# Gated cross-attention with a low-rank expert layer, on one core: evenly spread products for K and V, another order of the sums, and another tail

## The chip, the core and the metric

The kernel runs on one core of one Trainium2 chip. A core has engines that run beside each other, each with its own queue in order: TensorE (PE) multiplies matrices into eight PSUM banks; VectorE (DVE) does elementwise work and reductions; ScalarE (ACT) does activations and copies; GpSimd (POOL) does elementwise work on SBUF, more slowly; SyncE (SP) issues most DMAs. The metric is the device time of one execution in microseconds (us), the median of several. All data is float32, and a float32 matmul runs as two passes, so that each matmul of the code is two matmul records in the trace.

## What is computed

```python
x = x + tanh(g_xattn) * attention(layernorm(x), ctx)      # x: 4 x 256 x 512, ctx: 4 x 1601 x 512
x = x + tanh(g_ffn)  * ffn(layernorm(x))

q = (query @ Wq + bq)            # 32 heads of 128, 4 query heads for each of 8 key/value heads
k, v = split(kv @ Wkv + bkv)     # 8 heads of 128
attn = softmax(q k^T / sqrt(128)); o = attn @ v; attention = o @ Wo + bo
ffn = x @ base_W^T + 2 * sum over the two best of 8 experts of w_e * (x @ A_e) @ B_e     # rank 16
```

## The kernel before

The work runs over 4 batches, 8 key/value heads each, and l = 0, 1 for the two halves of the 256 queries: 64 **groups** (b, h, l). A group has four query heads for 128 queries, that is 512 columns. The 1601 keys lie in 13 tiles: 12 of 128 and one of 65. They are handled in 7 units, the odd tile first and then six pairs.

For a group, `score_unit` makes the scores of a unit on TensorE (keys on partitions, 512 columns), and ScalarE copies them from PSUM into a `p` buffer, of which there are NBUF = 9. VectorE folds the units into a maximum (`fold`, L766 to L772). When all 7 are there, `softmax` runs `spread` on VectorE, which takes the maximum over partitions by two 32 x 32 block transposes, two reductions, and six copies of 32 x 16 between quadrants of partitions (L785 to L799). Then come, unit by unit, a subtraction on VectorE (L870), exp on ScalarE (L873), and the sum over units on VectorE. `av_unit` multiplies with the values; its sum stands in the one bank of `ps_av`. `sum_spread` runs `spread` once more for the sums, with a reciprocal in it, and `normalize` divides (L961). Then ScalarE adds the bias of the values, and `out_steps` projects with `Wo` (L977); with the last head, `ffn_steps` follows.

`run_group(cur, prev)` lays the scores of one group between the value products of the one before. After it comes `window`, which fills TensorE while the maximum is spread. I call that stretch the **filling** behind a group. What goes in are `Task`s: q of the next head (four items), K and V of the next pair of heads, the projection of the previous group, transposes of the next batch's context, x and feed-forward steps. Each task has steps with a cost and a time of readiness, and some have a due group, from which `window` works out a credit.

K and V of a pair of heads are made by `pair_steps` with seven products of half size in place of eight (Strassen-Winograd): sums of context columns (`ctx_sums`, tile `T`, VectorE) and of weights (`weight_sums`, four additions on GpSimd, L291) go in, and the results are copied by ScalarE and added up by VectorE (L676). V is made for two heads in one tile `v`, one buffer; weights of K and of V share one buffer `wkv`.

Order is written by the program. `manual_schedule` keeps TensorE, VectorE and ScalarE in the order in which the code issues their instructions. The code decides this order by a planner: `clock` holds a planned time for each engine, `queues` hold pieces of vector and scalar work with planned durations, `pump` issues the piece that can start first, and `force(key)` issues pieces until a certain one is out. A wait that the planner doesn't foresee stops everything behind it on that engine. Instructions of GpSimd and SyncE are placed by the framework.

Three places matter for what follows. Behind a group, before its accumulator is free, `av_unit` forces the spread of the sums and the normalization, ahead of the next maximum:

```python
        if j == NPAIR - 1 and key not in by_pe:
            force(("sums", key))
            normalize(key, force(("rb", key)))
```

V of a pair is due at once, behind the first group of the pair (h even, l = 0); K of the next pair is due over three groups (h even, l = 1, to h odd, l = 1). And the tail lays out the last group by itself: its scores, then everything that is left, then the two last groups' value products one after the other. In the tail the sums of the last two groups are made on TensorE with a matrix of ones (`su`), and the reciprocal is taken over 128 x 512 (L941).

Of the kernel before, what the change touches and what calls it, by code (L numbers as in the profile page):

```python
# [27 lines left out]
def flamingo_kernel(  # L28
# [89 lines left out]
    SEM = 200  # L118
    NEVER = math.inf
# [23 lines left out]

    def pump(until=NEVER, most=None):

        n = 0
        while most is None or n < most:
            heads = [(start_of(q[0]), i, q) for i, q in enumerate(queues.values()) if q]
            if not heads:
                return n  # L150
            start, _, q = min(heads)
            engine, ns, _, fn, key = q[0]
            if start == NEVER or start + min(ns, 1200) / 2 > until:
                return n
            q.popleft()
            fn()
            clock[engine] = start + ns
            if key is not None:
                done[key] = start + ns + SEM
            n += 1  # L160
        return n

    def force(key):

        while key not in done:
            assert pump(most=1), key
# [27 lines left out]
    bias = const.tile([NBIAS, P], F32, name="bias")  # L194
    biasT = const.tile([P, NBIAS], F32, name="biasT")

    def load_small():
        nc.scalar.dma_start(bias[0:NHEAD], bq.rearrange("(h p) -> h p", p=P))
        nc.scalar.dma_start(bias[NHEAD:], bkv.rearrange("(h p) -> h p", p=P))
# [4 lines left out]
    def turn_bias():  # L204
        pb = bank("pb")
        nc.tensor.transpose(pb[:, :NBIAS], bias, ident[:NBIAS, :NBIAS])
# [50 lines left out]
    w_t = {}  # L257

# [24 lines left out]
    def weight_sums(kind, b, hp):  # L283
        w = w_t[kind, b, hp]
        for out_, x_, y_, op in (
# [5 lines left out]
            nc.gpsimd.tensor_tensor(w[:, out_], w[:, x_], w[:, y_], op)  # L291

# [50 lines left out]
    STAGE = 3  # L343

    LAG_DMA, LAG_CTX, LAG_X = 2500, 1500, 3000
# [178 lines left out]
    def new_v(b, hp):  # L524
        v_t[b, hp] = pool.tile([P, KT, 2, HDIM], F32, tag="v", name=f"v_{b}_{hp}", bufs=1)
# [40 lines left out]
    def plain_v_steps(b, hp):  # L566
# [3 lines left out]
        def item(i):  # L570
# [3 lines left out]
            def run():  # L574
                w = w_t["v", b, hp]
                pv = bank(f"pv_{b}_{hp}_{i}")
                for j in range(n):
# [14 lines left out]
                nc.scalar.copy(  # L592
                    v_t[b, hp][:r, i : i + n].rearrange("p j t f -> p (j t f)"), pv[:r, : n * WV]
                )
                give(act(585))
# [4 lines left out]
    def pair_steps(kind, b, hp):  # L600
# [48 lines left out]
        def places(f, half, s, n, bk):  # L649

            if is_k:
# [6 lines left out]
                    v_t[b, hp][:, lo : lo + n // P, f, :],  # L658
# [21 lines left out]
        def step(i, s, n):  # L680
# [24 lines left out]
            if i == 1:  # L705
                ready = ("T", b)
# [15 lines left out]
        def tail():  # L722
            over()
            bk = bank(f"pt{nm}")
            for f in range(2):
# [8 lines left out]
            nc.scalar.copy(  # L734
                v_t[b, hp][:REST, FULL].rearrange("p t f -> p (t f)"), bk[:REST, : 2 * HDIM]
            )
            give(act(400))

        def over():
            left[0] -= 1  # L740
            if not left[0]:
                done["pair", kind, b, hp] = clock["now"]

# [4 lines left out]
        else:  # L748
            new_v(b, hp)
            cols = [(HT + s, SUB) for s in range(0, HK, SUB)]  # L750
        parts = [[step(i, s, n) for i in (1, 2, 6, 7, 5, 3, 4)] for s, n in cols]
        if REST and not is_k:
            parts.append([(2 * NC * BLOCK_COST, ("T", b), tail, True)])
# [23 lines left out]
    def spread(acc, op, nm, after=None):  # L777
# [4 lines left out]
        res = pool.tile([P, W], F32, tag=f"res_{op}", name=f"res_{nm}", bufs=1)  # L782

        def quadrants():
# [3 lines left out]
            for a in range(1, 4):  # L788
                nc.vector.tensor_copy(q[:32, a, :], q[32 * a : 32 * a + 32, 0, :])

        def whole():
# [3 lines left out]
            for a in range(1, 4):  # L795
                nc.vector.tensor_copy(m[32 * a : 32 * a + 32], m[:32])

        def back():
# [4 lines left out]
        return res, [  # L803
            (690, lambda: nc.vector.tensor_tensor(acc[:, 0, :], acc[:, 0, :], acc[:, 1, :], op)),
            (710, lambda: nc.vector.transpose(acc[:, 1, :], acc[:, 0, :])),
            (1240, quadrants),
            (1070 if after is not None else 800, whole),
# [3 lines left out]
    def score_unit(key, j):  # L811
# [15 lines left out]
        else:  # L827
            p = pool.tile([P, 2, W], F32, tag="p", name=f"p_{nm}_{j}", bufs=NBUF)
# [19 lines left out]
    acc_t, sum_t, late = {}, {}, []  # L848
    last = (B - 1, NKV - 1, NL - 1)
    by_pe = [(B - 1, NKV - 1, l) for l in range(NL)]  # L850
    assert (NPAIR - 1) * 2 * W <= NC * 2 * HW

    def softmax(key):
# [4 lines left out]
        mb, parts = spread(acc_t[key], ALU.max, f"mx_{nm}")  # L858
        for ns, fn in parts:
# [21 lines left out]
        if key not in by_pe:  # L881
# [8 lines left out]
    def sum_spread(key):  # L890

        rb_t[key], parts = spread(
            acc_t[key],
            ALU.add,
            f"sm_{'_'.join(map(str, key))}",
            lambda m: nc.vector.reciprocal(m, m),
        )
        for i, (ns, fn) in reversed(list(enumerate(parts))):
            end = ("rb", key) if i == len(parts) - 1 else None
            queues["sum"].appendleft(("v", ns, 0.0, fn, end))  # L900
# [476 lines left out]
```

## Time and profile before

| what | value |
|---|---|
| median of 3 runs | 2723.4 us (2721.6 to 2724.55) |
| the profiled execution | 2725.56 us |
| its span, first to last instruction | 2723.8 us |
| mean granted TensorE clock | 0.985 |
| GpSimd: weight additions L291 | 60 for V, 88.4 us; 60 for K, 70.5 us |
| VectorE: copies of 32 x 16 for the sums (L789, L796) | 186 of 164 ns and 186 of 166 ns |
| VectorE: copies of 32 x 16 for the maximum | 192 of 164 ns and 192 of 166 ns |
| VectorE: reciprocal over 128 x 512 in the tail | 2 of 3358 ns |

Stretches of the span, from the profile's windows (columns: stretch, its length, busy time of each engine with its number of records, granted clock, share and rate of DMA):

```profile
0.00:74.00 74.00, 62.67 (x262) 45.62 (x263) 18.22 (x30) 17.80 (x35) 9.25 (x27) 1.00 0.37 123
74.00:110.00 36.00, 32.62 (x91) 16.54 (x92) 25.78 (x34) 21.05 (x32) 0.00 (x0) 0.91 0.22 63
640.00:705.00 65.00, 54.22 (x139) 27.39 (x137) 52.42 (x83) 24.54 (x37) 3.16 (x3) 0.89 0.08 25
2622.00:2724.00 102.00, 79.44 (x180) 34.80 (x178) 66.30 (x122) 27.91 (x40) 0.00 (x0) 0.88 0.05 16
110.00:640.00 530.00, 522.77 (x1810) 294.84 (x1809) 442.81 (x659) 242.74 (x386) 33.36 (x25) 1.00 0.12 39
```

The engines stand in the order PE, PEld (weight loads of TensorE), DVE, ACT, POOL. The first stretch is the start, up to the first scores; the second holds groups 0 and 1; the third is the change from the first batch to the second; the last is the tail. A wait is written as "who line <- whom line", with its sum, its number and the longest.

### The profile page before, as it was taken

How to read it: one execution, taken by the hardware profiler on the slowest of the kernel's cores; microseconds unless marked ns; L12 is line 12 of the kernel's file. 1: busy time of each engine (PE TensorE's matmuls, PEld its weight loads, DVE VectorE, ACT ScalarE, POOL GpSimd, SP SyncE). 2: the span in 40 equal slices, each digit the busy share in tenths (PEclk: the TensorE clock that was granted, in tenths of full speed). 3: DMA queues.
4: the chain of work that ended last, by engine and by line, in shares of the span. 5: the costliest groups of instructions: out<-in, count | busy, mean ns of one | idle time of the engine just before them, and what ended most of it. 6: DMA issues, size and time to landing. Idle time of an engine off the chain costs nothing.

```text
span 2723.8 us, 25225 instructions
## 1 busy us (share of the span) xinstructions
PE 2633.5 (97%) x9107; PEld 1486.4 (55%) x9107; DVE 2181.4 (80%) x3355; ACT 1207.4 (44%) x1898; POOL 165.7 (6%) x146
## 2 busy tenths in 40 slices
PE   8999999999999999999899999999989999999997
PEld 6546565564655646555365555656546564565643
DVE  2688787888778878788787887888877888888885
ACT  2444444445444344446354444454544444444441
POOL 0001000000000001000010000101000000000000
PEclk9999999999999999999899999999989999999998
DMA  3201001120111011102010111001110111111000
GB/s 128 61 24 38 31 24 39 39 88 0 39 43 39 24 43 47 31 24 87 16 47 22 36 51 39 24 31 42 57 39 24 35 32 35 39 33 37 24 16 8
DMA packets 78261, 104.70 MB, mean 38 GB/s; under 512 B 3324, under 2 KB 36140, under 8 KB 78136
## 3 DMA queue, kind: packets, MB, share of 16 engines
q1 hardware_dynamic: 76728, 102.01, 11.8%
q8 instruction: 72, 1.18, 0.2%
q0 software_dynamic: 272, 0.53, 0.1%
q10 hardware_dynamic: 1136, 0.55, 0.1%
q14 instruction: 53, 0.43, 0.0%
HBM read 100.98 MB, written 2.10 MB: 38 GB/s over the span
## 4 chain that ended last, share of the span: by engine, by line
PE 78%; DVE 16%; ACT 3%; issue 1%; DMA 1%; SPq 0%; ACTq 0%; DVEq 0%
PE av L912 21%; PE sc L834 20%; PE po L977 8%; PE pq L504 8%; PE pxk L629 5%; DVE p L870 3%; PE pyk L629 3%; DVE sm L772 3%; PE pyv L640 3%; ACT p L841 2%; DVE mx L772 2%; PE pxv L640 2%; PE pzk L629 1%; PE ptv L727 1%; PE py L1029 1%
## 5 line engine op out<-in xcount | busy, mean ns | idle before, releaser
L912 PE MATMUL av<-p,v 65*128 65x512 f32 x1640 | 775.1, 598 | 27.2 <-ACT p L873 27.2
L834 PE MATMUL sc<-qT,kT 128*128 128x512 f32 (+1 forms) x1664 | 782.4, 597 | 2.3 <-ACT qT L511 2.3
L841 ACT COPY p<-sc 65x512 f32<-65x512 f32 x820 | 467.9, 587 | 585.0 <-PE sc L834 417.9
L912 PEld LDWEIGHTS av<-p,v 65*128 65x128 f32 x1640 | 312.2, 192 | 412.1 <-issue 372.5
L834 PEld LDWEIGHTS sc<-qT,kT 128*128 128x128 f32 (+1 forms) x1664 | 309.7, 187 | 388.2 <-issue 361.7
L873 ACT ACTIVATE p<-p 65x512 f32<-65x512 f32 x442 | 428.1, 994 | 191.7 <-DVE p L870 187.3
L870 DVE TENSOR_TENSOR p<-p,res_mx 65x512 f32<-65x512 f32 x442 | 498.3, 1180 | 0.0
L772 DVE TENSOR_TENSOR mx<-mx,p 128x1024 f32<-128x1024 f32 x252 | 308.7, 1225 | 234.6 <-ACT p L841 231.0
L772 DVE TENSOR_TENSOR sm<-sm,p 128x1024 f32<-128x1024 f32 x252 | 316.2, 1255 | 7.2
L977 PE MATMUL po<-wo,oT 128*128 128x512 f32 x512 | 239.5, 612 | 15.2 <-DMA wo<-in_L_xattn_Wo_dram 12.4
L504 PE MATMUL pq<-xnT,wq 128*128 128x256 f32 x1024 | 235.0, 379 | 0.0
L504 PEld LDWEIGHTS pq<-xnT,wq 128*128 128x128 f32 x1024 | 193.5, 190 | 50.9 <-issue 18.4
L291 POOL TENSOR_TENSOR wv<-wv 128x256 f32<-128x256 f32 x60 | 88.4, 1492 | 1738.5 <-DMA wv<-in_L_xattn_Wkv_dram 1737.3
L667 ACT ACTIVATE kT<-pxk,biasT 128x384 f32<-128x384 f32 (+2 forms) x150 | 75.8, 526 | 264.4 <-PE pxk L629 264.4
L977 PEld LDWEIGHTS po<-wo,oT 128*128 128x128 f32 x512 | 98.9, 197 | 124.1 <-issue 113.9
L511 ACT ACTIVATE qT<-pq,biasT 128x256 f32<-128x256 f32 x128 | 60.5, 473 | 158.2 <-PE pq L504 158.2
L670 ACT COPY v<-pxv 128x384 f32<-128x384 f32 x120 | 56.5, 476 | 148.3 <-PE pxv L640 148.2
L766 DVE TENSOR_TENSOR mx<-p,p 128x1024 f32<-128x1024 f32 x63 | 77.5, 1230 | 48.7 <-ACT p L841 48.2
L291 POOL TENSOR_TENSOR wk<-wk 128x256 f32<-128x256 f32 x60 | 70.5, 1195 | 523.4 <-DMA wk<-in_L_xattn_Wkv_dram 397.0
L984 DVE SCALAR_TENSOR_TENSOR xa<-po,gates,xa 128x512 f32<-128x512 f32 x64 | 47.9, 749 | 62.5 <-PE po L977 62.4
L629 PE MATMUL pxk<-ctxT,wk 128*128 128x417 f32 (+1 forms) x240 | 90.5, 499 | 0.0
L640 PE MATMUL pxv<-wv,T 128*128 128x128 f32 x720 | 90.5, 276 | 0.0
(158 smaller groups left out, 2395.0 us busy)
## 6 DMA issues: line engine op xcount, KB each, us to landing
wq<-in_L_xattn_Wq_dram SPq DMA_DIRECT2D x32, 1024.0 KB, 5.2
wo<-in_L_xattn_Wo_dram SPq DMA_DIRECT2D x32, 1024.0 KB, 5.3
ctx<-in_ctx_dram SPq DMA_DIRECT2D x48, 256.0 KB, 2.7
wk<-in_L_xattn_Wkv_dram SPq DMA_DIRECT2D x30, 256.0 KB, 2.8
wv<-in_L_xattn_Wkv_dram SPq DMA_DIRECT2D x30, 256.0 KB, 3.0
xa<-in_x_dram SPq DMA_DIRECT2D x4, 512.0 KB
out_dram<-y SPq DMA_DIRECT2D x8, 256.0 KB, 2.0
base<-in_L_ffn_base_W_dram SPq DMA_DIRECT2D x4, 256.0 KB, 9.3
```

The costliest lines, as they stand in the source:

```text
L291: nc.gpsimd.tensor_tensor(w[:, out_], w[:, x_], w[:, y_], op)
L504: nc.tensor.matmul(pq[:, :L], w_t["q", b, h][:, c, g * HDIM : (g + 1) * HDIM], xnT_t[b][:, c, :], start=(c == 0), stop=(c == NC - 1),)
L629: nc.tensor.matmul(bk[:, :n], a(SLOT[i], c), operand(i, c, s, n), start=first and c == 0, stop=c == 1, skip_group_check=True,)
L640: nc.tensor.matmul(bk[:, t * HDIM : (t + 1) * HDIM], operand(i, c, s + t * P, P), a(SLOT[i], c), start=first and t == 0 and c == 0, stop=c ...
L766: nc.vector.tensor_tensor(acc, p[first], p[first + 1], op)
L772: nc.vector.tensor_tensor(acc, acc, p[j], op)
L834: nc.tensor.matmul(sc[:r, :], kT_t[b, h][:, key_col(i) : key_col(i) + r], qT_t[b, h][:, :, l * P : (l + 1) * P], start=True, stop=True,)
L841: nc.scalar.copy(p[:r, k, :], sc[:r, :])
L870: nc.vector.tensor_tensor(p, p, m, ALU.subtract)
L873: nc.scalar.activation(p, p, AF.Exp, scale=scale)
L912: nc.tensor.matmul(av, v_t[b, h // 2][:r, i, h % 2, :], p_t[key][j][:r, k, :], start=(j == 0 and k == 0), stop=(j == NPAIR - 1 and k == le ...
L977: nc.tensor.matmul(po, oT_t[key][:, g, :], w_t["o", b, h][:, g, :], start=(g == 0), stop=(g == G - 1),)
```

## The change

Seven things change together.

- **Sums.** `spread` gets an engine for its small copies: GpSimd for the sums, VectorE for the maximum as before. The planner lets 800 ns pass for three such copies (GP_COPIES). The spread result is written into the sums' own tile.
- **Normalization.** It is a piece in the queue of sums, forced only ahead of the next group's first value product.
- **The planner.** `force` finds the queue of the wanted piece, issues what stands before it there, and lets pieces of other queues of the same engine go first where they fit (FIT = 300).
- **K and V at an even rate.** V of the next pair is made from (h odd, l = 0) on and due by (h even, l = 0); chains share RATE = 10700 ns of TensorE in each filling, the older chain first. The next weights are loaded when the last product of the present ones is issued, and the products wait for them in the plan (LAG_PAIR). The values lie by head in a ring of three buffers. q of head 7 starts at l = 1.
- **Start.** K of the second head is a task in the first fillings.
- **Room.** Two staging buffers in place of three; the output is written over `x2`; `bias` lies in a buffer of `midT`.
- **Tail.** The last group's scores run between the value products of the one before (`run_group(last, prev, 4)`), its softmax starts as soon as they are out, and its value products are a task. Only the last group's sums are made on TensorE, and their reciprocal is taken on 128 x 16 between two transposes.

```diff
+    def take(q):
+        piece = q.popleft()
+        engine, ns, _, fn, key = piece
+        start = start_of(piece)
+        fn()
+        clock[engine] = start + ns
+        if key is not None:
+            done[key] = start + ns + SEM + (GP_COPIES if key[0] == "part" and key[2] < 4 else 0)
...
     def force(key):
         while key not in done:
-            assert pump(most=1), key
+            q = next((q for q in queues.values() if any(p[4] == key for p in q)), None)
...
+            engine, start = q[0][0], start_of(q[0])
+            for other in queues.values():
+                while other is not q and other and other[0][0] == engine:
+                    if start_of(other[0]) + other[0][1] > start + FIT:
+                        break
+                    take(other)
+            take(q)
...
-    STAGE = 3
-    LAG_DMA, LAG_CTX, LAG_X = 2500, 1500, 3000
+    STAGE = 2
+    LAG_DMA, LAG_CTX, LAG_X = 2500, 1700, 3000
...
-    def new_v(b, hp):
-        v_t[b, hp] = pool.tile([P, KT, 2, HDIM], F32, tag="v", name=f"v_{b}_{hp}", bufs=1)
+    def new_v(b, h):
+        v_t[b, h] = pool.tile([P, KT, HDIM], F32, tag="v", name=f"v_{b}_{h}", bufs=3)
...
             if i == 1:
-                ready = ("T", b)
+                ready = [("T", b), ("w", kind, b, hp)]
...
             for a in range(1, 4):
-                nc.vector.tensor_copy(q[:32, a, :], q[32 * a : 32 * a + 32, 0, :])
+                eng.tensor_copy(q[:32, a, :], q[32 * a : 32 * a + 32, 0, :])
...
-        rb_t[key], parts = spread(
+        rb_t[key] = acc_t[key][:, 0, :]
+        parts = spread(
             acc_t[key],
             ALU.add,
             f"sm_{'_'.join(map(str, key))}",
+            rb_t[key],
             lambda m: nc.vector.reciprocal(m, m),
+            nc.gpsimd,
         )
+        queues["sum"].appendleft(("v", 690, ("av", key), lambda: normalize(key), ("norm", key)))
         for i, (ns, fn) in reversed(list(enumerate(parts))):
-            end = ("rb", key) if i == len(parts) - 1 else None
-            queues["sum"].appendleft(("v", ns, 0.0, fn, end))
+            ready = 0.0 if i < 3 else ("part", key, i - 1)
+            queues["sum"].appendleft(("v", ns, ready, fn, ("part", key, i)))
...
+        if j == 0 and unfinished:
+            force(("norm", unfinished.pop()))
...
-        if j == NPAIR - 1 and key not in by_pe:
-            force(("sums", key))
-            normalize(key, force(("rb", key)))
+        if j == NPAIR - 1 and key != last:
+            done["av", key] = clock["now"] + SEM
+            unfinished.append(key)
...
-        nc.vector.reciprocal(rb, sum_t[key])
+        nc.vector.transpose(tr, sum_t[key])
+        give(vec(720))
+        nc.vector.reciprocal(m, tr.rearrange("p (c k) -> p c k", k=32)[:, :, 0])
+        nc.vector.transpose(
+            rb.rearrange("p (c k) -> p c k", k=32), m.unsqueeze(2).to_broadcast([P, NB, 32])
+        )
...
     def window(now):
+        left = RATE
...
+        for chain in sorted({t.chain for t in tasks if t.chain}):
+            some = [t for t in tasks if t.chain == chain]
+            cost = sum(t.cost() for t in some)
+            for t in some:
+                if t.due > now:
+                    t.credit = t.cost() * max(min(1, left / max(cost, 1)), 0)
+            left -= cost
...
-    for f in xs + vs + plain_k_steps(0, 1):
+    for f in xs + vs:
...
+    steps = plain_k_steps(0, 1)
+    steps.append((0, 0, lambda: last_sums(0)))
+    steps.append((0, 0, lambda: next_weights("k", 0, 1)))
+    tasks.append(Task(steps, 1))
...
-            if h % 2 == 0 and l == 0 and hi > 0:
-                tasks.extend(Task(part, now, True) for part in pair_steps("v", *pair))
...
-            if nxt is not None and l == (0 if nxt[1] > 0 else NL - 1):
+            if nxt is not None and l == (0 if 0 < nxt[1] < NKV - 1 else NL - 1):
                 tasks.append(Task(q_steps(*nxt), hi * NL + NL - 1))
...
+            if coming is not None and (h % 2, l) == (0, 1):
+                cb, cp = coming
+                steps = pair_steps("k", cb, cp, lambda c=coming: next_weights("v", *c))
+                tasks.append(Task(sum(steps, []), (hi | 1) * NL + NL - 1, now))
+            if coming is not None and (h % 2, l) == (1, 0):
+                cb, cp = coming
+                follow = next_pair(cb, cp)
+                then = None if follow is None else lambda f=follow: next_weights("k", *f)
+                for part in pair_steps("v", cb, cp, then):
+                    tasks.append(Task(part, (hi | 1) * NL + NL, now))
...
-    for j in range(NPAIR):
-        score_unit(last, j)
-    softmax(last)
-    flush(lambda t: True)
-    run_group(None, prev, 0)
-    tasks.insert(0, Task([sum_step(prev)] + out_steps(prev)))
-    run_group(None, last, 0, NEVER)
-    tasks.insert(0, Task(out_steps(last)))
+    run_group(last, prev, 4)
+    tasks.insert(0, Task(out_steps(prev)))
+    tasks.insert(0, Task([av_step(last, j) for j in range(NPAIR)] + out_steps(last)))
     flush(lambda t: True)
```

## The prediction

> **What bounds the kernel now.** I read the page's engine shares and chain first, then who TensorE waited for, then stretches of the timeline around the longest of these waits.
>
> ```profile
> span 2723.8 us, 25225 instructions
> PE 2633.5 (97%) x9107; PEld 1486.4 (55%) x9107; DVE 2181.4 (80%) x3355; ACT 1207.4 (44%) x1898; POOL 165.7 (6%) x146
> ...
> PE 78%; DVE 16%; ACT 3%; issue 1%; DMA 1%; SPq 0%; ACTq 0%; DVEq 0%
> ```
>
> TensorE bounds it, but 97% cannot be taken for a floor: records overlap and stretch when the clock falls. I count by starts instead. In undisturbed runs of the timeline a 512-column record starts every 0.429 us (eight of `po` at 864.12, the next at 867.56), a 256-column one every 0.216, a K product every 0.336 on average (0.350 and 0.322), a 128-column one every 0.112. The group list has 3950, 1128, 904 and some 3120 of them: 1695 + 244 + 304 + 349 = 2592 us. So 2723.8 - 2592 = 132 us is all that a better order can win. Where it lies, by TensorE's waits:
>
> ```profile
> PE av L912 <- ACT p L873: 27.2, 6, 6.5
> PE pyv L640 <- DVE v L676: 18.3, 12, 2.2
> PE po L977 <- DMA wo<-in_L_xattn_Wo_dram: 12.4, 3, 4.2
> PE pt_ctx L226 <- DMA ctx<-in_ctx_dram: 8.0, 4, 3.8
> PE pmt L1084 <- DVE mid L1074: 7.3, 2, 4.5
> PE pt_f L226 <- DVE fn L250: 4.8, 1, 4.8
> ```
>
> Columns: who, on whom, us in total, times, longest. The first and third row fall at the three batch boundaries. The first of them in the timeline:
>
> ```profile
> 643.79 1.45 PE L629 MATMUL pxk<-ctxT,wk 128*128 128x384 f32 x4
> 645.08 1.45 PE L629 MATMUL pzk<-ctxT,wk 128*128 128x384 f32 x4
> 646.38 2.74 PE L834 MATMUL sc<-qT,kT 128*65 128x512 f32 x6
> 655.64 2.08 PE L912 MATMUL av<-p,v 65*128 65x512 f32 x2 [6.53 <-ACT p L873]
> 657.51 3.62 PE L834 MATMUL sc<-qT,kT 128*128 128x512 f32 x4
> ...
> 685.74 1.45 PE L629 MATMUL pxk<-ctxT,wk 128*128 128x384 f32 x4
> 691.37 5.37 PE L977 MATMUL po<-wo,oT 128*128 128x512 f32 x8 [4.18 <-DMA wo<-in_L_xattn_Wo_dram]
> ```
>
> Behind group (head 7, l=0) the filling held only 5.4 us of K products (641.0 to 646.4), so TensorE ran dry for 6.5 us; after that four score records take 3.62 us where they take 1.88 elsewhere, the granted clock in 640 to 705 being 0.89. The projection postponed from there makes two projections in one filling, and the second waits 4.2 us for its weights.
>
> **The change part by part**, in us of span.
>
> *Products at an even rate.* Before, all V products of a pair (some 20 us) come behind one group, K in thirds behind three. After, both K and V are spread over all four fillings of a pair, at most 10.7 us each; K plus V of a pair is about 39.4 us by the starts above, or 9.9 per filling. In the burst, `pyv` accumulates and must wait for the vector add of an earlier part, which stood in VectorE's queue behind the sum and the maximum spread: 18.3 us in 12 waits. Half a burst with other pieces between has room for that add. Ends 0 and -18, taken **-14** (it is one wait per pair; I leave a quarter).
>
> *Batch boundary.* Per boundary: 6.5 of wait, 3.1 of slow records behind it (2.08, 3.62 and 2.22 against 1.02, 1.88 and 1.88), 4.2 for the weights of `po`, 1.8 of slow records: 15.6, or 47 for three. After, that filling gets K, and V of the next batch's first heads, to 10.7, plus a projection of 3.4; q of head 7 goes wholly into the filling before it. What is late next is the vector chain: in a usual boundary (855.3 to 866) sum spread 4.5, normalization 0.7, maximum spread 4.1, first subtraction 0.7 and exp 0.6, some 11 us. TensorE has the old group's last av records (3.4), the filling (14 and more) and three score tiles (2.6) against it: covered. The dry spell goes; the weights of `po` I count half gone, because the planner still knows no time for that load. 3 x (9.6 + 3.0) = **-38**, ends 0 and -47.
>
> *Start.* K of head 1 (10.8 us of products before the first scores) goes into the fillings behind groups 0 and 1, where TensorE waits 3.4 us for exp and then runs 4 score records in 3.62. **-6**, ends 0 and -8. Its weights load and additions are issued later with it, with a whole pair's time to spare.
>
> *Tail.* The four `su` records on the sums (1.7 us) go; two reciprocals over 128x512 of 3.36 us become transpose, small reciprocal, transpose (0.71 + 0.24 + 0.71 by their rows), for the last group; the other takes the usual path. Scores of the last group run between the av records of the one before, where TensorE now waits 1.3 and 3.0 us and then runs slow (2.9). The last serial piece (router, second product, output, from about 2697) stays. **-11**, ends -4 and -18.
>
> *Small copies on GpSimd.* Twelve copies of 0.165 us per group are on VectorE now; six move: 62 x 6 x 0.165 = 61 us of VectorE, which at 80% is not on the path, so nothing is gained directly. In exchange the second reduction and the last transpose each wait for three GpSimd copies, and behind a waiting vector instruction stand subtractions, maxima and the adds that K, V and ACT's score copies wait for. No such copy is in this trace; nearest are GpSimd memsets of 0.10 us, so three with their semaphores come to some 0.5 to 0.9 us. Here a rule speaks against the change. The row first:
>
> ```profile
> 70.26 2.89 POOL L291 TENSOR_TENSOR wk<-wk 128x256 f32<-128x256 f32 x4 [63.25 <-DMA wk<-in_L_xattn_Wkv_dram]
> ...
> 872.89 5.74 POOL L291 TENSOR_TENSOR wv<-wv 128x256 f32<-128x256 f32 x4 [116.20 <-DMA wv<-in_L_xattn_Wkv_dram]
> ```
>
> With VectorE idle four additions take 2.9 us; with VectorE on subtractions 5.7, and those subtractions go from 1.22 to 1.75. The Trainium skill, *SBUF — State Buffer*, "SBUF: two separate sides", says why: VectorE with two SBUF inputs and a GpSimd instruction that reads SBUF exclude each other for whole instructions. By the rule each of six copies could sit out one vector instruction of 1.2 us, 7.2 us per group of added latency; by the row, copies and vector instructions alternate only while VectorE has such an instruction ready, and as soon as it reaches the waiting reduction the copies run freely: one instruction of 1.2 us and then about 0.7, twice, or 3.8 per group less the 1.0 that the copies cost before, 2.8 us. The chain above is then 14 us against a cover of 20. I take the row: **+6** for the places where the cover is thin, ends 0 and +95 (1.5 in each of 63 groups).
>
> GpSimd also does the four weight additions for each of 30 loads (2 x 15), which stand until their DMA lands (3 us) and take 5.7. Copies behind them would come 6 to 9 us late, and the chain would be 20 to 23 against 20: it belongs to that upper end.
>
> *Normalization as a piece.* Its 0.69 us and the sum spread no longer have to come before the maximum spread, so exp of the next group can come up to 5 us earlier; but av's single accumulator makes the next group wait for it all the same. Counted within the boundary step.
>
> *Ring of three value buffers, split copies.* V of the next pair can start one group earlier than its last reader ends. ACT does 2 x 0.25 for 0.37 at each of 15 V ends, 2 x 0.37 for 0.56 at seven: about 3 us on an engine busy 44%. 0. *Two staging buffers for three:* a context load lands in 2.7 us and has two transposing steps of at least 1.7 between; 0, upper end +10. *Output in place of `y`:* 0.
>
> Sum: -14 - 38 - 6 - 11 + 6 = -63. On the profiled span, 2723.8 - 63 = 2661; its run was 2725.6, 1.8 around the span and 2.2 over the median of 2723.4. From the median: **2660**.
>
> **The rivals.**
>
> *Half of it* (0.22). The even rate works but the boundaries stay: context sums and K of the next batch become ready late, so the filling is bare whatever the rate allows, and `po` still meets its load. For it: 15.6 us at each boundary comes from readiness as much as from lack of work. Against: V is begun there too, where before it came a group later. -14 - 6 - 11 with +3: about 2695.
>
> *GpSimd turns the chain* (0.13, the other side). Place: the second reduction of the sums, VectorE waiting for copies which stand behind a vector instruction or behind weight additions whose DMA is not in. Price: what the chain exceeds its cover by. It decides from 69 us lost, 1.1 us per group over 63 groups, or 2.3 for each of 30 loads. For it: the rows above, and VectorE at 84% between 110 and 640. Against: the 6 us of cover to spare. At 1.5 per group: 2660 + 89 = 2749.
>
> *It does not spread* (0.06). Due dates and readiness push the products back into bursts; only the tail and a few us move: 2715, some of it within the bound for no change.
>
> **How the numbers follow.** My forecast has 0.59. A measurement of this kernel tells 0.2%, 5.4 us, from no change. Faster: 0.59 + 0.22 + half of the last, 0.84; same 0.03; slower 0.13. The range goes from 2632 (all the lower ends but some 10 us: 2592 of work, about 15 of filling the pipeline at the start, 20 of serial end) to 2712, which takes in the half case and costs of +50, and leaves out the slow side.
>
> **What would show it.** Right: no wait of `pyv` on VectorE's adds over 5 us in all; boundaries without a 6 us wait of `av` on exp and with clock 0.95 or more; tail from the last score record to the end shorter by 10; vector busy time down by about 60; `quadm` waits on GpSimd under 1 us each. Wrong: `av` or `sc` waiting about 1 us or more behind every group, released by a vector instruction that itself waited for GpSimd; GpSimd copies found behind the weight additions; or `po` still waiting for `wo` at each boundary.

## The result, and the profile after

The changed kernel takes 2961.3 us (median of 4 runs, 2958.1 to 2961.4), against 2722.7 us for the kernel before in the runs beside it: a ratio of 1.087, with a 95% interval of 1.085 to 1.089. The forecast was 2660. It is slower by 239 us where 63 less were expected.

The page of the changed kernel, its first lines and its chain:

```profile
span 2959.6 us, 25493 instructions
...
PE 2693.0 (91%) x9103; PEld 1501.9 (51%) x9103; DVE 2103.5 (71%) x2990; ACT 1210.5 (41%) x1914; POOL 219.5 (7%) x524
...
PE 83%; DVE 11%; POOL 3%; issue 1%; DMA 1%; ACT 1%; SPq 0%; POOLq 0%; DVEq 0%; ACTq 0%
```

TensorE has four records fewer than before and 236 us more of span. VectorE has become freer, as it should with the copies gone (2181 to 2104 us), and GpSimd is in the chain for the first time, with 3%. The busy time of TensorE is higher by 60 us for the same work, so a part of the loss is slow records. Who TensorE waited for tells where the rest is:

```profile
PE av L954 <- DVE oT L1005: 222.6, 37, 14.2
PE pt_x L249 <- DVE xn L273: 10.4, 4, 3.0
PE pt_ctx L249 <- DMA ctx<-in_ctx_dram: 6.9, 4, 3.5
PE av L954 <- ACT p L908: 4.7, 2, 2.6
```

One wait that did not exist before holds nearly the whole loss: value products of a group, 37 times, on `oT`, which is the normalization of the group before. The waits the change aimed at are gone from this list: `pyv` on VectorE (18.3), `po` on its weights (12.4), and most of `av` on exp (27.2).

To check that nothing else grew, I added up over the whole trace what lies between the start of a TensorE record and the next beyond the undisturbed spacing of its kind (0.429 us for 512 columns, and so on). The work itself is 2580 us before and 2578 after; the gaps are 136 and 374 us, a difference of 238. Gaps directly ahead of a group's first value product went from 28 to 231 us. Short ones, under 0.6 us, went from 36 to 93. Most of these lie where the clock was low: the trace has 33 stretches at half the clock, 279 us in all, where the kernel before has 12 with 84 us.

The place in the timeline, behind one ordinary group. Columns: start, duration, engine, line, operation, count, and in brackets the idle time before and what ended it.

```profile
198.03 0.68 DVE L835 TENSOR_TENSOR mx<-mx 128x512 f32<-128x512 f32 x1
...
201.61 0.71 DVE L829 STREAM_TRANSPOSE mb<-quadm_mx 128x512 f32<-128x512 f32 x1
...
203.53 1.81 DVE L905 TENSOR_TENSOR p<-p,mb 65x512 f32<-65x512 f32 x2
...
208.93 4.62 DVE L905 TENSOR_TENSOR p<-p,mb 128x1024 f32<-128x1024 f32 x4
...
212.43 2.79 PE L870 MATMUL sc<-qT,kT 128*65 128x512 f32 x6 [0.56 <-ACT qT L536]
212.56 4.08 POOL L315 TENSOR_TENSOR wv<-wv 128x256 f32<-128x256 f32 x4 [35.57 <-DMA wv<-in_L_xattn_Wkv_dram]
...
213.47 1.22 DVE L835 TENSOR_TENSOR sm<-sm 128x512 f32<-128x512 f32 x1
...
216.70 0.64 POOL L819 COPY quad_sm<-quad_sm 32x16 f32<-32x16 f32 x3
217.38 0.25 DVE L822 TENSOR_REDUCE quadm_sm<-quad_sm 32x16 f32<-32x64 f32 x1 [1.23 <-POOL quad_sm L819]
...
218.65 0.71 DVE L829 STREAM_TRANSPOSE sm<-quadm_sm 128x512 f32<-128x512 f32 x1 [0.75 <-POOL quadm_sm L826]
219.40 0.69 DVE L1005 TENSOR_TENSOR oT<-av,sm 128x512 f32<-128x512 f32 x1
...
220.14 2.08 PE L954 MATMUL av<-p,v 65*128 65x512 f32 x2 [4.92 <-DVE oT L1005]
```

VectorE's order is now: maximum spread (198.0 to 202.3), all seven subtractions with the additions of K between them (to 213.5), then the spread of the sums, then the normalization (done at 220.1). TensorE has run out of filling and of the three score tiles at 215.2. It stands for 4.9 us, though exp of the new group was ready since 204.9, and the two value records behind the wait take 2.08 us in place of 1.02. In the kernel before, the sums' spread and the normalization stood ahead of the maximum spread and of every subtraction (one place, from the normalization on):

```profile
821.37 0.69 DVE L961 TENSOR_TENSOR oT<-av,res_sm 128x512 f32<-128x512 f32 x1
...
821.98 0.68 DVE L804 TENSOR_TENSOR mx<-mx 128x512 f32<-128x512 f32 x1
...
827.20 1.80 DVE L870 TENSOR_TENSOR p<-p,res_mx 65x512 f32<-65x512 f32 x2
```

In the changed kernel all seven subtractions stand between the maximum spread and the normalization in each of 62 groups. In the place at 198 to 220 us the spread also pays for GpSimd: the copies start only when the four weight additions end at 216.64, about 0.5 us after their input was there.

Over all groups, from the end of a group's last value record (my reading of the two traces; minimum, median and maximum):

| | kernel before | changed kernel |
|---|---|---|
| maximum spread done | 5.1, 9.3, 13.4 us | before it to 6.9, median 4.0 us |
| normalization done | 0.9, 5.1, 9.2 us | 14.1, 21.8, 34.5 us |
| TensorE's work until the next group's first value record, median | 16.4 us | 18.8 us |

The normalization is later than TensorE's work in 38 of 63 places. The granted clock shows the second effect of the waits. From the windows, 110 to 640 us and 640 to 705 us (columns as in the table of before):

```profile
110.00:640.00 530.00, 499.97 (x1730) 282.05 (x1730) 393.44 (x536) 231.78 (x364) 46.96 (x101) 0.97 0.12 39
640.00:705.00 65.00, 44.50 (x100) 20.61 (x100) 42.60 (x69) 23.50 (x35) 1.13 (x6) 0.82 0.02 6
```

The steady stretch, at clock 1.00 before, has 0.97 and 80 records fewer. The batch boundary is worse than it was (0.82 for 0.89): there the longest wait, 14.2 us, ends at 653.9, because the sums of context columns (641.6 to 648.2) also stand ahead of the sums' spread on VectorE.

### The profile page after: what moved, and what is told of

Same layout as the page of the kernel before. It is cut to its first block, busy times and chain, and to the rows that moved or that the text cites. A ratio compares the mean times of both kernels' runs of the same rounds, so it can differ in the third digit from the quotient of the medians.

```text
span 2959.6 us, 25493 instructions
## 1 busy us (share of the span) xinstructions
PE 2693.0 (91%) x9103; PEld 1501.9 (51%) x9103; DVE 2103.5 (71%) x2990; ACT 1210.5 (41%) x1914; POOL 219.5 (7%) x524
## 4 chain that ended last, share of the span: by engine, by line
PE 83%; DVE 11%; POOL 3%; issue 1%; DMA 1%; ACT 1%; SPq 0%; POOLq 0%; DVEq 0%; ACTq 0%
PE av L954 25%; PE sc L870 22%; PE po L1020 7%; PE pxk L655 5%; PE pxv L666 5%; PE pq L529 5%; DVE p L905 4%; PE pyk L655 3%; PE pyv L666 3%; PE pzv L666 1%; PE pzk L655 1%; DVE sm L802 1%; PE py L1072 1%; DVE sm L829 1%; DVE oT L1005 1%
## 5 line engine op out<-in xcount | busy, mean ns | idle before, releaser
L954 PE MATMUL av<-p,v 65*128 65x512 f32 x1640 | 804.1, 617 | 227.3 <-DVE oT L1005 222.6
L877 ACT COPY p<-sc 65x512 f32<-65x512 f32 x820 | 474.3, 585 | 924.9 <-PE sc L870 799.3
L870 PE MATMUL sc<-qT,kT 128*128 128x512 f32 (+1 forms) x1664 | 821.4, 622 | 4.3 <-ACT qT L536 3.9
L870 PEld LDWEIGHTS sc<-qT,kT 128*128 128x128 f32 (+1 forms) x1664 | 324.7, 197 | 413.3 <-issue 391.7
L905 DVE TENSOR_TENSOR p<-p,mb 65x512 f32<-65x512 f32 x442 | 494.3, 1165 | 0.2
L1020 PE MATMUL po<-wo,oT 128*128 128x512 f32 x512 | 230.3, 592 | 0.0
L819 POOL COPY quad_sm<-quad_sm 32x16 f32<-32x16 f32 x189 | 36.3, 192 | 1759.6 <-DVE quad_sm L815 1753.8
L315 POOL TENSOR_TENSOR wv<-wv 128x256 f32<-128x256 f32 x60 | 71.8, 1216 | 477.5 <-DMA wv<-in_L_xattn_Wkv_dram 427.8
L666 PEld LDWEIGHTS pxv<-wv,ctxT 128*128 128x128 f32 x720 | 87.3, 192 | 15.0 <-issue 14.8
L655 PE MATMUL pxk<-T,wk 128*128 128x417 f32 (+1 forms) x240 | 90.5, 499 | 0.0
```

Of the source, the lines that this page charges most:

```text
L655: nc.tensor.matmul(bk[:, :n], a(SLOT[i], c), operand(i, c, s, n), start=first and c == 0, stop=c == 1, skip_group_check=True,)
L666: nc.tensor.matmul(bk[:, t * HDIM : (t + 1) * HDIM], operand(i, c, s + t * P, P), a(SLOT[i], c), start=first and t == 0 and c == 0, stop=c ...
L870: nc.tensor.matmul(sc[:r, :], kT_t[b, h][:, key_col(i) : key_col(i) + r], qT_t[b, h][:, :, l * P : (l + 1) * P], start=True, stop=True,)
L877: nc.scalar.copy(p[:r, k, :], sc[:r, :])
L905: nc.vector.tensor_tensor(p, p, m, ALU.subtract)
L954: nc.tensor.matmul(av, v_t[b, h][:r, i, :], p_t[key][j][:r, k, :], start=(j == 0 and k == 0), stop=(j == NPAIR - 1 and k == len(pairs[j]) ...
```

## Experiments

Theory O: the place of the sums' spread and the normalization in VectorE's order. Theory G: the copies on GpSimd. Theory F: the even rate leaves fillings too short. All ratios are against the kernel before, run on the same chip.

**Undo the order alone.**

```diff
         if j == NPAIR - 1 and key != last:
             done["av", key] = clock["now"] + SEM
-            unfinished.append(key)
+            force(("norm", key))
```

> After, with the sums' spread and the normalization forced again at the end of a group's value products, ahead of the next maximum. Theory O (order: the normalization stands behind the maximum and the subtractions on VectorE, and the one accumulator makes the next group's first value product wait for it): that wait, 222.6 us in 37 times, falls under 30, the clock goes back to 0.98 or more, 2640 to 2700 us. Theory G (GpSimd's copies delay the chain wherever it stands): the chain still comes late, now ahead of the maximum, so the next group waits for exp instead; 2850 to 2960. Theory F (evening out leaves fillings too short): 2800 or more, with waits before the first value product of the groups with l = 0.

2750.5 us, ratio 1.0099 (1.0084 to 1.0114). One line returns 211 of the 239 us; the wait of `av` on `oT` is gone. What takes its place, in the waits of this kernel:

```profile
PE av L954 <- ACT p L908: 72.1, 21, 5.3
```

Only 29 us of it lie at a group's first value product; 43 us, in 13 waits, lie between its own value products. Of these, 25 us are ahead of the last unit, and 17.8 us ahead of the last but one, once in each batch, in the group (head 6, l = 1). One place ahead of the last unit:

```profile
224.66 1.22 DVE L905 TENSOR_TENSOR p<-p,mb 128x1024 f32<-128x1024 f32 x1
...
225.91 1.06 ACT L908 ACTIVATE p<-p 128x1024 f32<-128x1024 f32 x1 [2.43 <-DVE p L905]
227.02 3.65 PE L954 MATMUL av<-p,v 128*128 128x512 f32 x4 [3.29 <-ACT p L908]
```

A last subtraction comes so late on VectorE (224.7) that its exp and the value product behind it wait: the vector queue runs behind by some 3 us at the end of the group.

**The copies alone, in the changed order.** `eng.tensor_copy` becomes `nc.vector.tensor_copy` in `spread`; the planner stays, and so does the order, record for record.

> After, with the six small copies of the sums on VectorE again and the order of everything else as it is. Theory O: within 30 us of 2961, the wait of av on the normalization still over 180 us. Theory G: the wait goes, 2700 or less.

2935.1 us in one run: 26 less than the changed kernel. The wait on `oT` is still 201.2 us in 37. GpSimd lengthens the late chain, it does not make it late.

**The accumulator.** Two banks for `ps_av` (six others in place of seven), and the normalization is forced only when two groups are unfinished, so it stays as late as in the changed kernel.

```diff
-        if j == 0 and unfinished:
-            force(("norm", unfinished.pop()))
+        if j == 0 and len(unfinished) > 1:
+            force(("norm", unfinished.pop(0)))
```

> After, with two PSUM banks for the value products in place of one (and six in place of seven for everything else), the normalization forced only ahead of the group after the next. Theory O: the wait of av on the normalization falls under 30 us and the time to 2640 to 2720, unless the missing bank costs something. Theory G: chain late all the same, waits move to the sums' tile and the score buffers, 2850 or more. Theory F: waits before the first value product stay, now for exp, 2800 or more.

2735.3 us, ratio 1.0047 (1.0030 to 1.0063). The median end of the normalization is 21.4 us after the last value record, as late as in the changed kernel, and TensorE no longer waits for it. So nearly all that the lateness costs, it costs through the single accumulator. The wait left is `av` on exp (45.1 us in 10), 8.4 us of it at each of the three boundaries.

**The copies alone, in the order of before.** The kernel before, with the sums' copies on GpSimd and nothing else; the order stays, record for record.

> Before, with the six small copies of the sums on GpSimd and nothing else, so that sums and normalization stay ahead of the maximum. Theory O: each group's chain gets 0.6 to 1.5 us longer, hidden by the filling except at the three batch boundaries and in the tail: 2720 to 2745. Theory G: over 2800.

2730.3 us, ratio 1.0023 (1.0014 to 1.0033): 7 us, close to the +6 of the prediction.

**Order by the queues.** Only the tuple of queue names is altered: `"sum"` stands first.

> The changed kernel with one line altered: the queue of sums stands first where two pieces of vector work could start at the same planned time (it stands behind the subtractions and the context sums in the changed kernel). Nothing is forced earlier. Theory O (what costs the time is only the place of the sums' spread and of the normalization in VectorE's order): they go out early again, the wait of av on the normalization falls from 223 us to under 40, time 2745 to 2790. Rival P (the planner does not count that wait, and everything it lays out afterwards is late): the order of ties alone leaves most of it, above 2880.

2774.2 us, ratio 1.0179 (1.0164 to 1.0194), inside what theory O gave; the wait on `oT` is 25.1 us in 5. The normalization now ends 8.0 us (median) after the last value record, and the maximum spread keeps its early place (3.2). That is the combination which the change could have had: both chains early, subtractions behind. It is 24 us slower than forcing the normalization first, so no gain from the early exp shows here. Part of that may be GpSimd: the sums' spread now stands among the subtractions, and the copies take twice as long as in the changed kernel (the changed kernel first, then this one):

```profile
L819 POOL COPY quad_sm<-quad_sm 32x16 f32<-32x16 f32 x189 | 36.3, 192 | 1759.6 <-DVE quad_sm L815 1753.8
L819 POOL COPY quad_sm<-quad_sm 32x16 f32<-32x16 f32 x189 | 73.4, 389 | 1804.4 <-DVE quad_sm L815 1600.3 <-DVE rie L1101 141.0 <-DVE rs_x L272 57.5
```

One place of this kernel, where the first of three copies waits for the subtraction to end:

```profile
196.51 1.15 DVE L905 TENSOR_TENSOR p<-p,mb 128x1024 f32<-128x1024 f32 x1
196.71 1.46 POOL L826 COPY quadm_sm<-quadm_sm 32x16 f32<-32x16 f32 x3 [1.90 <-DVE quadm_sm L933]
```

Of the 378 copies here, the 192 that met an idle VectorE took 0.19 us each, and the 46 beside a transpose, which reads one operand, took as long. The 50 that met a subtraction, which reads two SBUF operands, took 1.65 us in the median.

**The planner counts the wait.**

```diff
-            spend(len(pairs[j]) * mm_cost(W), force(("exp", key, j)))
-        if j == 0 and unfinished:
-            force(("norm", unfinished.pop()))
+            t = force(("exp", key, j))
+            if j == 0 and unfinished:
+                n = force(("norm", unfinished.pop()))
+                t = max(t, n) if key[:2] != last[:2] else t
+            spend(len(pairs[j]) * mm_cost(W), t)
```

> The changed kernel, in which the planner lets TensorE's planned time pass until the normalization is out before the next group's first value product (but for the last head). The order of the pieces is left to the queues. Theory P: with the wait in its plan the planner fills and orders rightly, time under 2800. Theory O: the pieces of the sums still stand behind seven subtractions, and TensorE waits for them as before: 2900 to 2965, the wait of av on the normalization above 170 us.

2828.4 us in one run, between the two theories; wait on `oT` 130.9 us in 27. Both missed: 133 us of the loss come back with this edit, while the pieces of the sums still stand behind seven subtractions in 57 of 62 groups. The traces show by what: the normalization comes 2.5 us earlier per group (19.1 us after the last value record in the median), and TensorE's work ahead of the next group's first value product is the same (1209 us in all for 1213). So this, too, acts mainly through the place of the normalization. The edit does two things at once: it lets planned time pass, and it forces the normalization before `spend` lets out more pieces. Which of them brings it forward was not separated.

**What else is in the remaining 28 us.** First the order of the first experiment, with the sums' copies on VectorE and planned there (GP_COPIES = -200, `nc.vector` in `sum_spread`):

> The kernel with the normalization forced at the end of the value products (2750.5 us), with the sums' small copies on VectorE, and planned there. What is left of the change: the even rate, the start, the tail, the room. Theory G (the copies on GpSimd hold the chain up by some 7 us over a kernel): 2741 to 2746, waits of av between its own products (26 us there) a little less. Theory F (the fillings behind head 6 are bare now, and late subtractions hold av up): still slower than the 2722.7 of before by 15 us or more. Rival: the copies were the whole of the rest, 2715 to 2725.

2719.7 us (10 runs), ratio 0.9978 (0.9966 to 0.9989). The rival holds: with the copies, the whole of the rest is gone. The step is 31 us here, not 7: the waits ahead of a group's last unit fell from 25 to 6 us. The other 17.8 us between a group's own value products stay. The 31 us are not the copies alone: the plan counts them anew, and the order on VectorE differs in many places, where it is the same in the two experiments on the copies alone. Theory G had the sign and less than a quarter of the size. Theory F, which asked for 15 us over the kernel before, falls, though its mechanism returns in small at the batch boundaries, below.

Then `force` as before, in the same kernel:

```diff
     def force(key):
         while key not in done:
...
+            assert pump(most=1), key
         return done[key]
```

> As the one before, with the planner's force of the kernel before: pieces are issued by earliest planned start until the wanted one is out, in place of the wanted piece's own queue first. Theory L (the new force holds the last subtractions of a group back behind sums and maxima): the waits of av between its own products fall from some 26 us to under 8, and the time to 2715 to 2728. Rival (they are late since the sums' spread stands ahead of the maximum's and the rest of VectorE's queue is as full as before): within 5 us of the one before.

2696.9 us, ratio 0.9896 (0.9882 to 0.9911): faster than the kernel before by 1.0%, and below what both theories gave. Theory L had the mechanism: the waits between a group's own value products, 23.5 us in 6 with the new `force`, are all gone. Its count of 26 us had left out those at (head 6, l = 1). There the last two subtractions stood behind the maxima of the next group in the kernel with the new `force`:

```profile
629.38 1.22 DVE L802 TENSOR_TENSOR mx<-mx,p 128x1024 f32<-128x1024 f32 x1 [1.22 <-ACT p L877]
630.52 2.35 DVE L905 TENSOR_TENSOR p<-p,mb 128x1024 f32<-128x1024 f32 x2
632.88 6.76 PE L954 MATMUL av<-p,v 128*128 128x512 f32 x8 [4.45 <-ACT p L908]
```

With the old `force` all seven of that group run together:

```profile
601.48 7.49 DVE L888 TENSOR_TENSOR p<-p,mb 65x512 f32<-65x512 f32 x7
```

Short gaps fall as well (my count, 44 to 28 us); first value products wait 4 us more, and `po` for its weights 8.0. The page and waits of this kernel:

```profile
span 2695.7 us, 25296 instructions
...
PE 2622.9 (97%) x9103; PEld 1483.1 (55%) x9103; DVE 2167.2 (80%) x3368; ACT 1212.7 (45%) x1920; POOL 153.7 (6%) x146
```

```profile
PE av L937 <- ACT p L891: 32.0, 7, 9.4
PE po L1003 <- DMA wo<-in_L_xattn_Wo_dram: 8.0, 3, 2.7
...
PE pyv L649 <- DVE v L685: 1.4, 1, 1.4
```

VectorE is as full as before the change (80%), and this is the better kernel: the 63 us of VectorE that the changed kernel saves were never on the path.

The copies again, on this base:

> The fastest so far (2696.9 us: normalization at the end of the value products, old force, sums' copies on VectorE), with the sums' copies back on GpSimd and planned there. Theory G (what the copies cost hangs on how tight the order is: 31 us with the new force, 7 in the kernel before): with the old force 2703 to 2712, and waits of av between its own products under 12 us. Rival (the copies cost some 30 us in any order that has the normalization at the end): 2724 to 2732, and these waits 20 us or more.

2707.7 us, ratio 0.9939 (0.9924 to 0.9954): 11 us, as theory G said, and no wait between a group's own value products. The plan and the order change in this pair too. And the old `force` alone in the changed kernel:

> The changed kernel with nothing altered but force, which issues by earliest planned start again until the wanted piece is out; the normalization stays a piece that is forced ahead of the next group's first value product, the copies stay on GpSimd. Theory O (the spread and the normalization go out late since they stand behind seven subtractions, whichever force is used): 2920 to 2965, wait of av on the normalization above 180 us. Rival L (the new force puts the subtractions first; by planned start the sums would come earlier): under 2850.

2939.8 us, ratio 1.0791 (1.0775 to 1.0807), wait on `oT` 209.2 in 37. The new `force` costs some 22 us in either order, and is not the cause of the large loss. Here it costs them another way: with it the normalizations end 17 us later in all, and the wait on `oT` is 13 us longer.

**The even rate alone.** The fastest kernel so far, with V of a pair in one burst behind its first group and K in shares by due time. In my edit V's products come behind q and projections in that filling.

```diff
-                tasks.append(Task(sum(steps, []), (hi | 1) * NL + NL - 1, now))
+                tasks.append(Task(sum(steps, []), (hi | 1) * NL + NL - 1))
-            if coming is not None and (h % 2, l) == (1, 0):
...
-                    tasks.append(Task(part, (hi | 1) * NL + NL, now))
+            if hi > 0 and (h % 2, l) == (0, 0):
...
+                    tasks.append(Task(part, now))
```

> The fastest so far, with the products laid as in the kernel before: V of a pair all behind its first group, K in shares by due time over three groups. What is left of the change: start, tail, room, split copies. Theory E (the even rate is worth what the prediction said, some 14 us in pyv waits and part of 38 at the boundaries): 2709 to 2725, pyv waits back at 15 us or more. Rival (the gain of the fastest is the tail and the start, some 12 us, and the ends of the pyv waits are spent elsewhere): within 5 us of 2696.9.

2690.5 us, ratio 0.9876 (0.9859 to 0.9892), the fastest of all. Theory E falls: without the even rate the kernel is some 6 us faster, and the `pyv` waits do not come back (2.6 us in 4). But three things differ from the kernel with the even rate: the burst, V's place behind q and projections, and K's, which also stands behind them in my edit. The last run puts V's products first in the filling, as the kernel before had them (`Task(part, now, 1)`); K's stay behind:

> The kernel with V in bursts again (2690.5 us), in which V's products go ahead of projections and q in the filling, as the kernel before has it. Theory W (pyv waited in the kernel before because V's products came first in the filling, when VectorE still had the spreads ahead of their additions; not because they came in one burst): the pyv waits return to 10 us or more, 2699 to 2712. Rival (the burst is short of waits because of the value ring and its split copies): pyv waits stay under 5 us, within 4 us of 2690.5.

2695.6 us, ratio 0.9896 (0.9879 to 0.9912), 5 us more than behind the others. The waits of this kernel:

```profile
PE av L937 <- ACT p L891: 23.3, 4, 7.3
PE pyv L649 <- DVE v L685: 15.9, 8, 2.2
```

The waits are back, the time is a little under what theory W gave. They come from the place of V's products in the filling, while VectorE still has the spreads ahead of their additions, and not from the burst. And with V first in the filling, burst (2695.6) and even rate (2696.9) take the same time: the even rate saves these waits and gives them back elsewhere (`av` on exp 32.0 for 23.3, `po` on its weights 8.0 for none). What K's place adds, no run shows.

## Why the prediction was wrong

The runs divide the difference of 239 us in four steps, each the difference of two kernels:

| from | to | us |
|---|---|---|
| before, 2723 | normalization first, old `force`, copies on VectorE, 2697 | -26 |
| old `force` | new `force`, 2720 | +23 |
| copies on VectorE | on GpSimd, with the plan for it, 2751 | +31 |
| normalization first | as a late piece, 2961 | +211 |

**The step that failed** is "Normalization as a piece". It saw the mechanism ("av's single accumulator makes the next group wait for it all the same") and priced it at nothing, "counted within the boundary step". There the chain was taken from a place of the kernel before: sum spread, normalization, maximum spread, subtraction, exp, some 11 us, 14 with GpSimd, against a cover of 20. Both terms were off. The changed kernel's chain ends with the normalization and has seven subtractions (8.2 us) and additions of K in it, where the sum counted one: median 21.8 us. The cover is 18.8 us in the median, and less behind many groups. I kept the old order of VectorE in mind while the change made it free. It could be read in the code: the piece is forced only after the exp of the next group, and the queue of subtractions wins a tie. 37 waits of 6.0 us on average are 222.6; short gaps, most of them at the lower clock behind the waits, added some 57; the waits that went away, 53, come off, and 10 of `pt_x` on VectorE are new. The second accumulator and the undone order show it from two sides, and `"sum"` first in ties from a third.

**Small copies on GpSimd**, +6. In the order of before it is 7, and the single cost was right: three copies take 0.64 us, with VectorE standing 0.75 to 1.2 us for them in the timeline shown. But the cost depends on what is late around it: 26 us in the changed order, and, with the plan and the order altered too, 11 with the old `force` and 31 with the new one. The prediction's two ends, 0 and 95, hold all four; its value was that of the mildest order. Taken as one lost instruction for each copy, the Trainium skill's rule of whole instructions excluding each other (*SBUF — State Buffer*, "SBUF: two separate sides") would have made 7.2 us per group of it, by estimate some 450 us over 63; the row was nearer, since VectorE mostly stood idle when the copies ran (345 of 378 in the changed kernel). Where it did not, the trace agrees with the rule: 1.65 us beside a subtraction and 0.19 beside a transpose, in the kernel with `"sum"` first.

**The planner's new `force`**, +22, does not appear in the prediction at all, so it was put at nothing without a reason. It is a change of the order of VectorE's and ScalarE's work: with the normalization first it leaves subtractions behind the next group's maxima (23.5 us of waits), in the changed order it makes the normalization later.

**Products at an even rate**, -14. The `pyv` waits went as forecast (18.3 to 1.4 in the fastest kernel with it), but they go as well in a burst that stands behind the other work of its filling, which is 6 us faster; and against a burst in their own place the even rate gains nothing (2696.9 and 2695.6), since the boundaries take it back.

**Batch boundary**, -38. In the kernel with the order undone and the old `force`, almost nothing of it comes: the gaps of TensorE over the three boundaries are 63 us for 64 before, `av` on exp is 32.0 us (27.2 before), `po` on its weights 8.0 (12.4). With V spread ahead, the first filling behind head 6 has only part of V left and the second no products (work of 13.0 and 14.2 us up to the first value product, where the burst puts 26.4 in the first). K of the next batch still waits for its context sums, so the filling behind (head 7, l = 0) gets 8.4 us of K where the prediction put 14 of K, V and a projection. This is the rival "half of it", whose argument was right; but it left out both the order and `force`.

**Start**, -6: it came. Up to the first scores nothing is gained (gaps 12.9 us before, 14.3 in that kernel), but the gain was forecast behind groups 0 and 1, and up to the first value product of group 2 the gaps go from 21.4 to 15.5. **Tail**, -11: gaps 28.8 to 22.6 and 1.7 us of records gone, so -8, within its ends. In the changed kernel itself the tail has 31.8 us of gaps, since the last groups wait for the normalization too. Start, tail and boundaries together leave some -14 of that kernel's 28 us for the stretches between, where the even rate was given -14. So 2697 near the rival's 2695 is more than luck.

The rival on the other side named GpSimd in this chain and 2749. It had the chain and the cover in the right place, and the wrong thing in the chain. Its sign, copies found behind the weight additions, was there as well (216.64 in the timeline), and yet with the copies on VectorE the wait on `oT` stayed at 201 us. The range's lower end, 2632, is all the lower ends in full and not all but 10 us. Left open: which half of planning for the wait brings the normalization forward, what K's place in the filling is worth, and why `po` stops waiting for its weights in the burst kernels.

## What to carry to other kernels

Where one buffer links two groups, the piece that frees it has a deadline: before it is made movable, list everything that may now be issued ahead of it on its engine, and hold that sum against the work that covers it. Unloading an engine that was not the bound bought nothing here and lengthened a chain through it. When several edits come together, revert the order first, then the rest one by one: here a change that was 8.7% slower held a version 1.0% faster than the original.

## What the runs showed of the hardware

Three 32 x 16 copies between quadrants on GpSimd take 0.64 us, hardly more than the 0.52 us on VectorE, when VectorE is idle; handing over and back adds 0.16 us in the median of the changed kernel, so VectorE stands 0.81 us for a set of three. Beside a VectorE instruction with two SBUF operands a copy can take far longer: with `"sum"` first in ties, 50 copies that met a subtraction took 1.65 us in the median, 46 beside a transpose 0.19. GpSimd is slower at the same work: four additions of 128 x 256 take it 2.9 us with VectorE idle, 0.72 each, where VectorE takes 0.42 for one. A wait of TensorE costs more than itself: behind the 4.9 us wait two records took 2.08 us for 1.02, and over the changed kernel the short gaps grew by 57 us beside 223 us of waits, while the mean granted clock fell from 0.985 to 0.953.
